# An edge MLP with segment maximum: two groups of short matmuls at other places between the tiles, and gathers held nearly one by one

## The chip, the cores and the metric

One core of a Trainium2 chip. The metric is the device time of one execution of the program, in microseconds (us); the time of the kernel before is the median of three runs.

## What is computed

A graph has N = 12500 nodes with 32 features and E = 400000 edges, sorted by their target node. Each edge takes the normalised features of its source and its target and 32 features of its own through a two-layer MLP; each node keeps the maximum of what its incoming edges give.

```python
h = jnp.maximum(_layernorm(x, axis=-1), 0.0)
e_feat = jnp.concatenate([h[src], h[dst], edge_attr], axis=-1)   # 96 wide
v = jax.nn.relu(e_feat @ W1 + b1) @ W2 + b2                      # 64, then 32
x_cand = jax.ops.segment_max(v, dst, num_segments=N)
return x + jnp.maximum(x_cand, h)
```

## The kernel before

The edges are cut into four stripes of 100000, and each stripe into 196 chunks of 512 edges; a chunk c is the same 512 positions in all four stripes. The main loop (L854) takes two chunks c and c+1 per iteration, a **pair**, through both layers, prepares the two chunks a = c+2 and b = c+3, and finishes the span products of the pair before. What TensorE (PE) does in one iteration, with the names that the profile gives (output <- operands):

- **ea**, `edges_into` (L773, ph<-ea,wt): the edge features times their part of W1, into four banks of PSUM.
- **of**, `windows_into` (L773, ph<-of,qf): what the target nodes give to layer 1, as spans of rows of q times a one-hot mask `of`, which ScalarE (ACT) builds (L641, L642). Added into the same banks.
- **ht**, `rows_into` (L773, ph<-ht,wt): the gathered source rows, transposed by VectorE (DVE), times their part of W1. Added into the same banks. ACT's relu follows (L798).
- **tr**, `leave_1` (L669): transposes of the running maxima of the pair before.
- **a1, a2, a3**, `tile` (L344, pv<-hs,hot): tiles of node spans. One in four of the source rows isn't gathered by DMA but picked by matmul: a one-hot matrix `hot` times the node features `hs`, 14 matmuls a tile; DVE masks and reduces the result (L351, L352). A chunk has four tiles, MM = 4; tile a0 was made in the iteration before, where it is called n0.
- **l2**, `second_layer` (L807).
- **lv**, `leave_2` (L686): span products, which bring the maxima of the pair before to the rows of their nodes. ACT copies one half of the result (`wo`, L692), DVE adds the other (`leave_3`, L700), and SyncE (SP) sends the stripes' rows to DRAM.
- **b0 to b3**, again L344, and in 34 of the chunks b an extra tile (pv<-hs,zero and xg), whose one-hots DVE builds late (L274).
- **n0**, tile 0 of the next pair's chunk a.

The trace holds two records for each f32 matmul of ea, of, ht and l2, so eight instructions show as x16.

GpSimd (POOL) only starts gathers: 24 indirect DMAs a pair (L179, 23 where the chunk has the extra tile), each of 128 rows of the node features from DRAM, for the pair two iterations on. POOL takes them in program order, and a table **HELD** paces them: its key is the gather's position in its pair (0 to 23), its value how many iterations back, and behind which **milestone** of PE, the gather may start. `passes` notes the matmul that is a milestone, `hold` puts the gather behind it by a semaphore, and gathers without an entry follow the one before them. In the kernel before, the table has 12 entries, two gathers to a milestone. A buffer of a gather holds three of them and there are 14; PSUM has a ring of seven banks.

Of the kernel before, what the change touches and what calls it, by code (L numbers as in the profile page):

```python
# [39 lines left out]
NCH = 196  # L40
# [6 lines left out]
A1 = 7  # L47
# [16 lines left out]
LATE = NCH - 8  # L64
PIECE = 2 * A0
GP = 3
HELD = {0: (3, 'b1'), 2: (3, 'b2'), 4: (3, 'b3'), 6: (3, 'n0'), 8: (2, 'ea'), 10: (2, 'ht'), 12: (2, 'tr'), 14: (2, 'a1'), 16: (2, 'a2'), 18: (2, 'a3'), 20: (2, 'lv'), 22: (2, 'b0')}
BANKS = 7
SOON = {(3, 0): 'a0', (3, 6): 'a2', (4, 0): 'a3', (4, 6): 'b0', (5, 0): 'b1', (5, 6): 'b2'}
ROUND = 12582912.0  # L70
# [13 lines left out]
def gnn_kernel(ctx, tc, x, src, src_mm, src_x, src_t, dst, dst_ext, lo, lo_c, ends_b, edge_attr, weights, w1, w2, b2, out):  # L84
# [129 lines left out]
    def passes(iteration, name, ins):  # L214

        passed[iteration, name] = ins

    def hold(c, i, ins):

        at = HELD.get(i + c % 2 * (K - MM))  # L220
        if at and c // 2 - at[0] >= 0:
# [9 lines left out]
    def bank(name):  # L231

        return ring[0].tile([P, C], F32, name=name, tag="bank", bufs=BANKS)
# [94 lines left out]
    def tile(c, m):  # L328

        if c not in MMC or m == MM and c not in MMX:  # L330
            return
        if m == 0:
            mm_rows[c] = early.tile([P, MM, D], F32, name="gm", bufs=4)
        if m < MM:
            hot = [hots[c][:, k, m * P:(m + 1) * P] for k in range(A1)]
            mask, row = masks[c][:, m], mm_rows[c][:, m]
        else:
            _, mask, spaces = extras.pop(c)
            hot = [spaces[k // 2][:, k % 2 * P:(k % 2 + 1) * P] for k in range(A1)]
            row = gh[c][-1][:, SOME - 1]  # L340
        po = bank("pv")[:, :D * A0]
        for k in range(A1):
            for part in range(2):
                ins = nc.tensor.matmul(po, hot[k], hs[:, part, k].rearrange("p f a -> p (f a)"),  # L344
                                 start=(k == 0 and part == 0), stop=(k == A1 - 1 and part == 1))
        if m == 0 and c % 2 == 0:
            passes(c // 2 - 2, "n0", ins)
        passes(c // 2 - 1, "ab"[c % 2] + str(m), ins)
        of_group = po.rearrange("p (f a) -> p f a", a=A0)
        one = early.tile([P, D, A0], F32, name="one", bufs=2)  # L350
        nc.vector.tensor_tensor(one, of_group, mask[:, None, :].to_broadcast([P, D, A0]), op=ALU.mult)  # L351
        nc.vector.tensor_reduce(row, one, axis=AX.X, op=ALU.max)  # L352
# [3 lines left out]
    def to_features(c, part):  # L356

        if c >= NCH or (c, part) in turned:
            return
        turned.add((c, part))  # L360
        if c not in hts:
            hts[c] = early.tile([P, K, D], F32, name="ht", bufs=4)
        ht = hts[c]
        n = min(K - MM * (c in MMC), (SE - c * C) // D)
        if part < J:
            r = slice(part * SOME, min((part + 1) * SOME, n))
            if r.start < n:
                nc.vector.transpose(ht[:, r].rearrange("p k e -> p (k e)"),  # L368
                                    gh[c][part][:, :r.stop - r.start].rearrange("p k f -> p (k f)"))
        elif c in MMC:  # L370
            nc.vector.transpose(ht[:, n:].rearrange("p k e -> p (k e)"),
                                mm_rows.pop(c).rearrange("p k f -> p (k f)"))
        else:
            for k in range(J, len(gh[c])):
                r = slice(k * SOME, min((k + 1) * SOME, n))
                nc.vector.transpose(ht[:, r].rearrange("p k e -> p (k e)"),
                                    gh[c][k][:, :r.stop - r.start].rearrange("p k f -> p (k f)"))
            if n < K:
                nc.vector.memset(ht[:, n:], 0.0)
# [183 lines left out]
    with tc.tile_pool(name="edges", bufs=3) as pool, tc.tile_pool(name="edges_ps", bufs=1, space=PSUM) as ps:  # L563
# [90 lines left out]
        def blocks(c):  # L654
            return min(J, -(-(SE - c * C) // P))
# [23 lines left out]
        def leave_2(c, sos, last):  # L679

            n = 1 + (c < NCH - 2)
            pw = bank("pv")[:, :n * 2 * P]
            pw = pw.rearrange("p (x h q) -> p x h q", x=n, h=2)
            for x in range(2):
                for j in range(blocks(c + x)):
                    ins = nc.tensor.matmul(pw[:, x % n], last[x][:, j].rearrange("p s w -> p (s w)"),  # L686
                                           sos[x][0][:, j], start=(j == 0 and x < n),
                                           stop=(j == blocks(c + x) - 1 and x >= 2 - n))
            passes(c // 2 + 1, "lv", ins)
            wo = pool.tile([P, 2, P], F32, name="wo", bufs=2)  # L690
            if c < NCH - 6:
                nc.scalar.activation(wo, pw[:, :, 0], AF.Copy)  # L692
            else:
                nc.vector.tensor_copy(wo[:, :n], pw[:, :, 0])
            return pw, wo
# [80 lines left out]
        def edges_into(c):  # L776

            ph = banks[c] = [bank("ph") for s in range(NS)]
            passes(c // 2, "ea", into_ph(ph, [(w1c, loaded[c + x][0]) for x in range(2)], True, False))
            return ph  # L780

        def windows_into(c, ph):
            of = [ofs.pop(c + x) for x in range(2)]
            q = fetched.pop(c // 2)
            into_ph(ph, [(q[:, x], of[x]) for x in range(2)], False, False)
# [40 lines left out]
        tile(2, 0)  # L826
        one_hots(3, 0, 2)
        tile(2, 1)
        one_hots(3, 2, BY_ACT.start)
        mask_of(3)  # L830
# [10 lines left out]
        ph = edges_into(0)  # L841
# [11 lines left out]
        windows_into(0, ph)  # L853
        for c in range(0, NCH - 4, 2):  # L854
            a, b = c + 2, c + 3
            if c:
                ph = edges_into(c)
                windows_into(c, ph)
            rows_into(c, ph)
            if c % LOAD:  # L860
                load_edges(c + LOAD // 2 + AHEAD)
# [7 lines left out]
            if c == LATE + 2:  # L869
                ea = pool.tile([P, LOAD * C], F32, name="ea", bufs=2)  # L870
# [3 lines left out]
            if c:  # L874
                so = [leave_1(c - 2 + x, sbs[x]) for x in range(2)]
# [15 lines left out]
                tile(a + 2, 0)  # L891
            pv = second_layer(c, hid)
            if c:
                pw = leave_2(c - 2, so, last)
            if c:
                one_hots_act(a + 2)
            load_keys(a + KEYS)
            load_key_x(b + 2)
# [7 lines left out]
            sms = [scan(c, pv[0], sm)]  # L906
            if c:
                tile(b, 0)
                to_features(b, 0)
            sms.append(scan(c + 1, pv[1], sms[0]))  # L910
            sm = sms[1]
# [10 lines left out]
            last = [lasts(c + x) for x in range(2)]  # L922
# [27 lines left out]
            tile(b, MM)  # L950
            to_features(b, 3)
            to_features(b, J)
            if a + 2 < NCH - 2:
                if c:
                    tile(a + 2, 0)
            else:
                ph = edges_into(c + 2)
                windows_into(c + 2, ph)
            if a + 2 < NCH - 2:
                to_features(a + 2, 0)  # L960
            if c == (NB - 1) * BLOCK + 2:
                bp = bank("pv")[:, 0:1]
# [31 lines left out]
        c = NCH - 4  # L994
# [5 lines left out]
        so = [leave_1(c - 2 + x, sbs[x]) for x in range(2)]  # L1000
# [6 lines left out]
        ph = edges_into(c + 2)  # L1007
        windows_into(c + 2, ph)
        pw = leave_2(c - 2, so, last)
# [4 lines left out]
        so = [leave_1(c + x, sbs[x]) for x in range(2)]  # L1014
# [9 lines left out]
        pw = leave_2(c, so, lasts_2[:2])  # L1024
# [9 lines left out]
        so = [leave_1(c + 2 + x, sbs[x]) for x in range(2)]  # L1034
# [152 lines left out]
```

## Time and profile before

| | us |
|---|---|
| runs, median (lowest, highest) | 3587.91 (3581.08, 3589.38) |
| profiled execution | 3575.96 |
| its span, first to last instruction | 3574.1 |
| PE busy | 3241.7 (91%) |
| DVE busy | 2223.2 (62%) |
| POOL busy | 2207.4 (62%) |
| ACT busy | 1578.5 (44%) |

The profile is of one execution. A row of a group gives line, engine, operation, output and operands, shape and count, then busy time and the mean of one in ns, then the idle time of the engine just before such instructions and what ended most of it. "issue" there means that the engine stood still and the profile shows nothing that it waited for. In rows by time, the first two numbers are start and length in us; a run of like instructions is one row, and brackets at its end give the idle time ahead of it. The granted clock is the share of TensorE's full clock that the chip allowed, 1.00 at full speed. Busy time of PE is modelled at its ends, since matmuls overlap.

### The profile page before, as it was taken

How to read it: one execution, taken by the hardware profiler on the slowest of the kernel's cores; microseconds unless marked ns; L12 is line 12 of the kernel's file. 1: busy time of each engine (PE TensorE's matmuls, PEld its weight loads, DVE VectorE, ACT ScalarE, POOL GpSimd, SP SyncE). 2: the span in 40 equal slices, each digit the busy share in tenths (PEclk: the TensorE clock that was granted, in tenths of full speed). 3: DMA queues.
4: the chain of work that ended last, by engine and by line, in shares of the span. 5: the costliest groups of instructions: out<-in, count | busy, mean ns of one | idle time of the engine just before them, and what ended most of it. 6: DMA issues, size and time to landing. Idle time of an engine off the chain costs nothing.

```text
span 3574.1 us, 55458 instructions
## 1 busy us (share of the span) xinstructions
PE 3241.7 (91%) x19141; PEld 2547.7 (71%) x19141; DVE 2223.2 (62%) x4215; ACT 1578.5 (44%) x2470; POOL 2207.4 (62%) x2337
## 2 busy tenths in 40 slices
PE   5899999989999998999999999989999999999987
PEld 3577777777777776777777767777777777777765
DVE  5456666666666666666666666656665666666655
ACT  3344444443534444444443434444444444444443
POOL 6666666665666666666666666666666666666662
PEclk8899999999999999999999999999999999999997
DMA  5322222222222222222222222222222222222222
GB/s 175 99 60 62 53 64 62 62 50 62 64 62 53 61 63 65 50 66 60 62 50 70 57 56 58 59 59 61 60 62 59 60 61 61 63 65 49 59 58 65
DMA packets 178819, 227.49 MB, mean 64 GB/s; under 512 B 109621, under 2 KB 150373, under 8 KB 165734
## 3 DMA queue, kind: packets, MB, share of 16 engines
q10 hardware_dynamic: 29828, 108.01, 9.6%
q0 software_dynamic: 74336, 38.21, 8.5%
q1 hardware_dynamic: 74370, 77.70, 7.0%
q8 instruction: 151, 2.47, 0.3%
q14 instruction: 134, 1.10, 0.1%
HBM read 212.23 MB, written 11.46 MB: 63 GB/s over the span
## 4 chain that ended last, share of the span: by engine, by line
PE 81%; issue 10%; DVE 6%; another core or an unknown queue 2%; SPq 1%; DMA 1%; ACT 1%; DVEq 0%; ACTq 0%
PE pv L344 60%; PE ph L773 10%; PE pv L686 4%; PE pv L669 3%; PE pv L807 3%; DVE hot L304 1%; DVE one L351 1%; DVE last L650 1%; DVE sm L815 1%; DMA top_d<-wo 0%; DVE ht L368 0%; SPq L616 0%; SPq L707 0%; SPq L625 0%
## 5 line engine op out<-in xcount | busy, mean ns | idle before, releaser
L179 POOL DMA_INDIRECT gh<-h_d,src_i x2291 | 2169.8, 947 | 1296.3 <-issue 560.0
L344 PE MATMUL pv<-hs,hot 128*128 128x448 f32 x10752 | 2373.0, 378 | 97.5 <-issue 83.9
L344 PEld LDWEIGHTS pv<-hs,hot 128*128 128x128 f32 x10752 | 2089.1, 196 | 345.7 <-issue 159.7
L351 DVE TENSOR_TENSOR one<-pv,mask 128x448 f32<-128x448 f32 x768 | 472.3, 615 | 1219.7 <-remote 464.7
L798 ACT ACTIVATE hid<-ph,wt 128x512 f32<-128x512 f32 x392 | 250.0, 688 | 1124.6 <-remote 498.2
L352 DVE TENSOR_REDUCE gm<-one 128x32 f32<-128x448 f32 x768 | 476.2, 620 | 26.5
L304 DVE TENSOR_TENSOR hot<-kb,consts 128x1024 fp32r<-128x1024 f16 (+1 forms) x379 | 447.5, 1199 | 0.0
L318 ACT ACTIVATE hot<-away,ones 128x512 fp32r<-128x512 f32 x582 | 421.6, 724 | 45.0 <-remote 26.1
L317 ACT ACTIVATE away<-kb,key_n 128x512 f32<-128x512 f16 x582 | 416.0, 715 | 0.0
L692 ACT ACTIVATE wo<-pv 128x256 f32<-128x256 f32 x95 | 36.6, 385 | 631.2 <-remote 439.2
L815 DVE TENSOR_TENSOR_SCAN sm<-pb,sm,pv 128x512 f32<-128x512 bf16 x195 | 243.6, 1249 | 16.5 <-remote 9.0
L686 PEld LDWEIGHTS pv<-so,last 128*128 128x128 f32 x768 | 107.5, 191 | 159.5 <-issue 148.5
L773 PE MATMUL ph<-ht,wt 32*64 32x512 f32 x1568 | 197.3, 618 | 21.0 <-issue 13.0
L686 PE MATMUL pv<-so,last 128*128 128x256 f32 x768 | 148.6, 304 | 74.3 <-issue 67.7
L368 DVE STREAM_TRANSPOSE ht<-gh 128x96 f32<-128x96 f32 x774 | 207.4, 269 | 1.2
L661 ACT ACTIVATE sb<-sm,wt 128x512 f32<-128x512 f32 x196 | 138.1, 715 | 138.7 <-issue 87.6
L669 PEld LDWEIGHTS pv<-ident,sb 128*128 128x128 f32 x782 | 91.8, 150 | 120.3 <-issue 95.1
L773 PE MATMUL ph<-of,qf 32*64 32x512 f32 x1552 | 147.6, 600 | 19.6 <-issue 17.5
L669 PE MATMUL pv<-ident,sb 128*128 128x128 f32 x782 | 126.4, 298 | 30.4 <-issue 24.4
L773 PEld LDWEIGHTS ph<-ht,wt 32*64 32x64 f32 x1568 | 62.7, 135 | 114.1 <-issue 98.5
L642 ACT ACTIVATE of<-of,ones 128x512 f32<-128x512 f32 x194 | 140.6, 725 | 6.3
L641 ACT ACTIVATE of<-db,below 128x512 f32<-128x512 int32 x194 | 137.4, 708 | 0.0
(115 smaller groups left out, 1328.2 us busy)
## 6 DMA issues: line engine op xcount, KB each, us to landing
ea<-in_edge_attr SPq DMA_DIRECT2D x49, 1024.0 KB
db<-in_dst_ext ACTq DMA_DIRECT2D x48, 1024.0 KB
gh<-h_d,src_i POOLq DMA_INDIRECT x2291
pb<-pen_d ACTq DMA_DIRECT2D x48, 512.0 KB
kb<-key_d ACTq DMA_DIRECT2D x47, 512.0 KB
top_d<-wo SPq DMA_DIRECT2D x752, 3.0 KB
qf<-q_d SPq DMA_DIRECT2D x392, 16.0 KB
q_d<-qs SPq DMA_DIRECT2D x6, 512.0 KB
```

The source lines that it names most:

```text
L179: ins = nc.gpsimd.indirect_dma_start(out=parts[-1][:, i, :], out_offset=None, in_=h_d[:, :], in_offset=bass.IndirectOffsetOnAxis(ap=src_i[ ...
L304: nc.vector.tensor_tensor(hot_of(c)[:, start:stop], keys[c][:, None, :].to_broadcast([P, n, MM * P]), key_ps[:, start:stop, None].to_broad ...
L317: nc.scalar.activation(away, keys[c], AF.Square, bias=key_n[:, k:k + 1])
L318: nc.scalar.activation(hot_of(c)[:, k], away, AF.Relu, bias=ones, scale=-1.0)
L344: ins = nc.tensor.matmul(po, hot[k], hs[:, part, k].rearrange("p f a -> p (f a)"), start=(k == 0 and part == 0), stop=(k == A1 - 1 and par ...
L351: nc.vector.tensor_tensor(one, of_group, mask[:, None, :].to_broadcast([P, D, A0]), op=ALU.mult)
L352: nc.vector.tensor_reduce(row, one, axis=AX.X, op=ALU.max)
L669: passes(c // 2 + 1, "tr", nc.tensor.transpose(px[:, j, :], sb[:, j * P:(j + 1) * P], ident))
L686: ins = nc.tensor.matmul(pw[:, x % n], last[x][:, j].rearrange("p s w -> p (s w)"), sos[x][0][:, j], start=(j == 0 and x < n), stop=(j == ...
L773: ins = nc.tensor.matmul(ph[s][x * HID:(x + 1) * HID], w[g], e[g], start=start, stop=stop)
L798: nc.scalar.activation(hid[k], of, AF.Relu, bias=b1c)
L815: nc.vector.tensor_tensor_scan(found[:, :n], loaded.pop(c)[2][:, :n], pv[:, :n], -LOW if before is None else before[:, C - 1:C], op0=ALU.a ...
```

## The change

Four things, with no instruction of an engine added or removed:

1. HELD goes from 12 to 21 entries: nearly every gather has a milestone of its own.
2. A tile is a milestone twice: at its end as before, and in its middle (name with "-").
3. ea and of of the next pair move from the head of an iteration to the end of the one before, ahead of n0 instead of behind it.
4. lv moves from right behind l2 to behind b0, and with it the ACT copy of its result, past the three one-hot halves (six instructions) that ACT builds for the next chunk a (`one_hots_act(a + 2)`) and the loads behind them.

Lines behind the table move by 2 and those behind `tile` by 4: L344 becomes L346, L669 L673, L686 L690, L692 L696, L773 L777, L807 L811, L179 L181.

```diff
--- before.py
+++ after.py
@@ -64,7 +64,9 @@
 LATE = NCH - 8
 PIECE = 2 * A0
 GP = 3
-HELD = {0: (3, 'b1'), 2: (3, 'b2'), 4: (3, 'b3'), 6: (3, 'n0'), 8: (2, 'ea'), 10: (2, 'ht'), 12: (2, 'tr'), 14: (2, 'a1'), 16: (2, 'a2'), 18: (2, 'a3'), 20: (2, 'lv'), 22: (2, 'b0')}
+HELD = {0: (3, 'b1'), 1: (3, 'b2-'), 2: (3, 'b2'), 3: (3, 'b3-'), 4: (3, 'b3'), 5: (2, 'ea'), 6: (3, 'n0-'),
+        7: (3, 'n0'), 9: (2, 'ht'), 10: (2, 'tr'), 12: (2, 'a1-'), 13: (2, 'a1'), 14: (2, 'a2-'), 15: (2, 'a2'),
+        16: (2, 'a3-'), 17: (2, 'a3'), 18: (2, 'l2'), 19: (2, 'b0-'), 20: (2, 'b0'), 21: (2, 'lv'), 22: (2, 'b1-')}
 BANKS = 7
 SOON = {(3, 0): 'a0', (3, 6): 'a2', (4, 0): 'a3', (4, 6): 'b0', (5, 0): 'b1', (5, 6): 'b2'}
 ROUND = 12582912.0
@@ -343,9 +345,11 @@
             for part in range(2):
                 ins = nc.tensor.matmul(po, hot[k], hs[:, part, k].rearrange("p f a -> p (f a)"),
                                  start=(k == 0 and part == 0), stop=(k == A1 - 1 and part == 1))
-        if m == 0 and c % 2 == 0:
-            passes(c // 2 - 2, "n0", ins)
-        passes(c // 2 - 1, "ab"[c % 2] + str(m), ins)
+            if k in (A1 // 2, A1 - 1):
+                at = "" if k == A1 - 1 else "-"
+                if m == 0 and c % 2 == 0:
+                    passes(c // 2 - 2, "n0" + at, ins)
+                passes(c // 2 - 1, "ab"[c % 2] + str(m) + at, ins)
         of_group = po.rearrange("p (f a) -> p f a", a=A0)
         one = early.tile([P, D, A0], F32, name="one", bufs=2)
         nc.vector.tensor_tensor(one, of_group, mask[:, None, :].to_broadcast([P, D, A0]), op=ALU.mult)
@@ -853,9 +857,6 @@
         windows_into(0, ph)
         for c in range(0, NCH - 4, 2):
             a, b = c + 2, c + 3
-            if c:
-                ph = edges_into(c)
-                windows_into(c, ph)
             rows_into(c, ph)
             if c % LOAD:
                 load_edges(c + LOAD // 2 + AHEAD)
@@ -891,8 +892,6 @@
                 tile(a + 2, 0)
             pv = second_layer(c, hid)
             if c:
-                pw = leave_2(c - 2, so, last)
-            if c:
                 one_hots_act(a + 2)
             load_keys(a + KEYS)
             load_key_x(b + 2)
@@ -906,6 +905,7 @@
             sms = [scan(c, pv[0], sm)]
             if c:
                 tile(b, 0)
+                pw = leave_2(c - 2, so, last)
                 to_features(b, 0)
             sms.append(scan(c + 1, pv[1], sms[0]))
             sm = sms[1]
@@ -950,13 +950,11 @@
             tile(b, MM)
             to_features(b, 3)
             to_features(b, J)
+            ph = edges_into(c + 2)
+            windows_into(c + 2, ph)
             if a + 2 < NCH - 2:
                 if c:
                     tile(a + 2, 0)
-            else:
-                ph = edges_into(c + 2)
-                windows_into(c + 2, ph)
-            if a + 2 < NCH - 2:
                 to_features(a + 2, 0)
             if c == (NB - 1) * BLOCK + 2:
                 bp = bank("pv")[:, 0:1]
```

On PE, one pair from tr on, up to tr of the next pair, before (64x512 is one instruction of L773; x56 is b0 to b3):

```order
L669 MATMUL pv<-ident,sb 128x128 x8
L344 MATMUL pv<-hs,hot 128x448 x42
L807 MATMUL pv<-hid,wt 32x512 x8
L686 MATMUL pv<-so,last 128x256 x8
L344 MATMUL pv<-hs,hot 128x448 x56
L344 MATMUL pv<-hs,zero 128x448 x4
L344 MATMUL pv<-hs,xg 128x448 x10
L344 MATMUL pv<-hs,hot 128x448 x14
L773 MATMUL ph<-ea,wt 64x512 x8
L773 MATMUL ph<-of,qf 64x512 x8
L773 MATMUL ph<-ht,wt 64x512 x8
L669 MATMUL pv<-ident,sb 128x128 x8
```

The same stretch after:

```order
L673 MATMUL pv<-ident,sb 128x128 x8
L346 MATMUL pv<-hs,hot 128x448 x42
L811 MATMUL pv<-hid,wt 32x512 x8
L346 MATMUL pv<-hs,hot 128x448 x14
L690 MATMUL pv<-so,last 128x256 x8
L346 MATMUL pv<-hs,hot 128x448 x42
L346 MATMUL pv<-hs,zero 128x448 x4
L346 MATMUL pv<-hs,xg 128x448 x10
L777 MATMUL ph<-ea,wt 64x512 x8
L777 MATMUL ph<-of,qf 64x512 x8
L346 MATMUL pv<-hs,hot 128x448 x14
L777 MATMUL ph<-ht,wt 64x512 x8
```

lv (L686, now L690) stands behind the first 14 of the tiles of b, and the last tile, n0, stands between of and ht instead of ahead of ea.

On ACT, where the copy wo stood before, among the six one-hot halves of an iteration (away and hot, three halves for chunk b and three for the next a):

```order
L318 ACTIVATE hot<-away,ones 128x512
L692 ACTIVATE wo<-pv 128x256
L317 ACTIVATE away<-kb,key_n 128x512
```

and after, at the end of the same six:

```order
L319 ACTIVATE away<-kb,key_n 128x512
L320 ACTIVATE hot<-away,ones 128x512
L287 DMA kb<-key_d 128x2048
L696 ACTIVATE wo<-pv 128x256
L665 ACTIVATE sb<-sm,wt 128x512 x2
```

The copy wo stood between the third half and the fourth, and stands now behind all six and behind the load of keys, ahead of the running maxima's bias (sb).

On POOL, eight gathers of a pair with what each waits for (DMASW: a queue slot of an earlier gather; DVE: its buffer; PE: a milestone), before:

```order
L179 DMA gh<-h_d,src_i 128x32 [waits DMASW2_49,DVE_49,PE_49]
L179 DMA gh<-h_d,src_i 128x32 [waits DMASW3_49]
L179 DMA gh<-h_d,src_i 128x32 [waits DMASW4_49,PE_49]
L179 DMA gh<-h_d,src_i 128x32 [waits DMASW5_49,DVE_49]
L179 DMA gh<-h_d,src_i 128x32 [waits DMASW6_49,PE_49]
L179 DMA gh<-h_d,src_i 128x32 [waits DMASW7_49]
L179 DMA gh<-h_d,src_i 128x32 [waits DMASW0_49,DVE_49,PE_49]
L179 DMA gh<-h_d,src_i 128x32 [waits DMASW1_49]
```

and after:

```order
L181 DMA gh<-h_d,src_i 128x32 [waits DMASW2_49,DVE_49,PE_49]
L181 DMA gh<-h_d,src_i 128x32 [waits DMASW3_49,PE_49]
L181 DMA gh<-h_d,src_i 128x32 [waits DMASW4_49,PE_49]
L181 DMA gh<-h_d,src_i 128x32 [waits DMASW5_49,DVE_49,PE_49]
L181 DMA gh<-h_d,src_i 128x32 [waits DMASW6_49,PE_49]
L181 DMA gh<-h_d,src_i 128x32 [waits DMASW7_49,PE_49]
L181 DMA gh<-h_d,src_i 128x32 [waits DMASW0_49,DVE_49,PE_49]
L181 DMA gh<-h_d,src_i 128x32 [waits DMASW1_49,PE_49]
```

Every gather of these now waits for PE, where every second one did.

## The prediction

> **What bounds the kernel now.** I read the page's busy times and chain first.
>
> ```profile
> PE 3241.7 (91%) x19141; PEld 2547.7 (71%) x19141; DVE 2223.2 (62%) x4215; ACT 1578.5 (44%) x2470; POOL 2207.4 (62%) x2337
> ...
> PE 81%; issue 10%; DVE 6%; another core or an unknown queue 2%; SPq 1%; DMA 1%; ACT 1%; DVEq 0%; ACTq 0%
> ...
> L179 POOL DMA_INDIRECT gh<-h_d,src_i x2291 | 2169.8, 947 | 1296.3 <-issue 560.0
> L344 PE MATMUL pv<-hs,hot 128*128 128x448 f32 x10752 | 2373.0, 378 | 97.5 <-issue 83.9
> ...
> L686 PE MATMUL pv<-so,last 128*128 128x256 f32 x768 | 148.6, 304 | 74.3 <-issue 67.7
> ```
>
> TensorE (PE) sets the end; next comes "issue", PE standing still for nothing that the profile names. The waits of PE say where:
>
> ```profile
> PE pv L344 <- issue: 90.9, 172, 2.7
> PE pv L686 <- issue: 67.7, 130, 1.1
> PE ph L773 <- issue: 40.5, 44, 14.8
> PE pv L344 <- DVE zero L274: 27.1, 15, 3.0
> PE pv L669 <- issue: 24.4, 44, 1.1
> ...
> PE pv L344 <- DVE hot L304: 12.2, 10, 2.7
> ...
> PE pv L344 <- DVE mask L323: 3.0, 2, 2.6
> ```
>
> L686 (lv, span products), L669 (tr, transposes) and L773 (ea, of, ht) are short matmuls, and lose more than their share: L686 has 768 records to L344's 10752, yet loses 67.7 us to its 90.9. (The 27.1 us for zero are the extra tile's wait for DVE in some of the pairs; the change leaves it as it is.) To see why I read one pair in PE's order of time (start, length, line, tiles, count, idle before):
>
> ```profile
> 2025.62 2.96 PE L344 MATMUL pv<-hs,hot 128*128 128x448 f32 x14
> 2028.51 1.11 PE L773 MATMUL ph<-ea,wt 32*64 32x512 f32 x16
> 2029.42 1.06 PE L773 MATMUL ph<-of,qf 32*64 32x512 f32 x16
> 2030.28 1.06 PE L773 MATMUL ph<-ht,wt 32*64 32x512 f32 x16
> 2031.27 1.09 PE L669 MATMUL pv<-ident,sb 128*128 128x128 f32 x8
> ...
> 2041.14 1.09 PE L807 MATMUL pv<-hid,wt 64*32 64x512 f32 x16
> 2042.16 0.97 PE L686 MATMUL pv<-so,last 128*128 128x256 f32 x6
> 2043.62 0.37 PE L686 MATMUL pv<-so,last 128*128 128x256 f32 x1 [0.48 <-issue]
> 2045.03 0.28 PE L686 MATMUL pv<-so,last 128*128 128x256 f32 x1 [1.04 <-issue]
> 2046.42 0.91 PE L344 MATMUL pv<-hs,hot 128*128 128x448 f32 x2 [1.11 <-issue]
> ...
> 2063.45 1.11 PE L773 MATMUL ph<-ea,wt 32*64 32x512 f32 x16
> 2065.22 2.75 PE L773 MATMUL ph<-ht,wt 32*64 32x512 f32 x16
> ```
>
> A tile of node spans takes 2.89 us (2025.62 to 2028.51), ea 0.91, of 0.86, ht 0.99, tr 0.85, l2 1.02. Here lv with b0's first matmul loses 0.48 + 1.04 + 1.11 = 2.63 us; the later ht takes 2.75 where the earlier took 1.06: 1.69 lost. Beside lv runs this on POOL:
>
> ```profile
> 2028.86 0.95 POOL L179 DMA_INDIRECT gh<-h_d,src_i  x1 [4.65 <-PE pv L344]
> ...
> 2035.01 0.94 POOL L179 DMA_INDIRECT gh<-h_d,src_i  x1 [1.46 <-remote]
> ...
> 2043.77 0.94 POOL L179 DMA_INDIRECT gh<-h_d,src_i  x1 [0.30 <-issue]
> 2046.75 0.94 POOL L179 DMA_INDIRECT gh<-h_d,src_i  x1 [2.04 <-PE pv L686]
> ```
>
> Eight gathers in a row, 0.95 + 0.30 = 1.25 us each, from 2035.01; PE is free again after the last. Another pair, PE then POOL:
>
> ```profile
> 2157.60 1.22 PE L686 MATMUL pv<-so,last 128*128 128x256 f32 x8
> 2158.66 7.59 PE L344 MATMUL pv<-hs,hot 128*128 128x448 f32 x36
> ```
>
> ```profile
> 2154.37 0.95 POOL L179 DMA_INDIRECT gh<-h_d,src_i  x1 [1.25 <-PE pv L344]
> ```
>
> POOL had paused 1.25 us shortly ahead of that lv, and it loses nothing. Of the 84 lv from 360 to 3400 us, 68 had POOL without a pause of note in the 4 us before and lost 3.05 us on average (lv with b0's first ten matmuls); 16 had a pause, and lost 0.06. First and last of the stalled, then of the clean:
>
> ```profile
> 396.01 0.86 PE L686 MATMUL pv<-so,last 128*128 128x256 f32 x5
> ...
> 3260.40 0.86 PE L686 MATMUL pv<-so,last 128*128 128x256 f32 x5
> ```
>
> ```profile
> 502.05 1.25 PE L686 MATMUL pv<-so,last 128*128 128x256 f32 x8
> ...
> 3299.03 1.22 PE L686 MATMUL pv<-so,last 128*128 128x256 f32 x8
> ```
>
> So I hold that short matmuls pile up something that a long run of gathers keeps from draining, and that a pause of POOL of about 1 us drains. The trace shows the coincidence, not the mechanism. A stall costs twice: by stretches (length; busy time of PE, PEld, DVE, ACT, POOL; granted clock),
>
> ```profile
> 2042.20:2046.40 4.20, 1.58 (x13) 1.39 (x9) 0.00 (x0) 0.00 (x0) 1.90 (x3) 0.86 0.11 16
> 2046.40:2051.00 4.60, 4.58 (x13) 4.05 (x13) 3.92 (x6) 2.79 (x5) 3.34 (x4) 0.50 0.12 20
> ```
>
> the 4.6 us behind this one run at a clock of 0.50. Over the whole run the clock is
>
> ```profile
> core 0: 3574.1 us, clock 0.944
> ```
>
> so (1 - 0.944) x 3574 = 200 us go to it, beside 90.9 + 67.7 + 25.7 + 24.4 = 208.7 us of issue waits (25.7 is 40.5 without its one wait of 14.8, a single stretch of no pair): about 1 us of clock per us of stall, if all of it follows stalls.
>
> **The change part by part.** No instruction is added or removed, so POOL still needs 24 x 1.25 = 30.0 us a pair; the pair above, 2028.51 to 2063.45, took 34.9, which leaves it 4.9 us of pauses. What changes is where they fall, and what PE does then. All terms are for some 97 pairs.
>
> 1. *The waits of tile n0 for DVE.* The 12 waits for hot and mask (15.2 us, longest 2.7) stand at n0, ahead of which DVE builds n0's one-hots. Now ea and of stand there, 0.91 + 0.86 = 1.77 us: all but the longest are covered. -14; bounds -15 and 0.
>
> 2. *Span products behind b0.* Until now 24 short matmuls in a row (l2, lv); now 16, then a tile of 2.89 us, then 8. Records per time fall, but POOL is no freer. By the new holds each half tile (1.44 us) releases one gather (1.25), so POOL works off 0.2 us per half tile; what n0, ht and tr release (gathers 7 to 11, 6.25 us, within the 0.99 + 0.85 + 1.44 = 3.3 us to the middle of a1) leaves 3 us of backlog, and through l2 and b0 POOL still runs without a pause. I take about half of L686's 67.7, because the burst is split and not relieved: -35. Bounds: -68 (all gone) and +68 (lv stalls alike, and b0 behind l2 anew).
>
> 3. *ht and tr.* They now follow n0, not of. b3, ea and the middle of n0 release one gather each, 3.75 us, in 0.91 + 0.86 + 1.44 + 1.44 = 4.6 us from b3's end to n0's, so POOL pauses just ahead of them. Half of L773's 25.7 and L669's 24.4: -25; bounds -50 and 0.
>
> 4. *ea and of.* They leave the end of n0 for the end of b3, where gathers 22, 23 and 0 to 4, 7 x 1.25 = 8.75 us, are released over the 7.2 us from the middle of b1 to b3's end: no pause ahead of them. The nearest row is the stalled ht, 1.69 us; 97 of these would be +164, none 0. Today L773 waits 44 times, several to a burst, so about one burst in four of one kind; one in four here is 24 x 1.69 = +41. ACT's span masks for of are early enough to be read 2.89 us sooner; the last of the pair above ended at 2018.55, 10.9 us ahead of its matmuls:
>
> ```profile
> 2017.82 0.73 ACT L642 ACTIVATE of<-of,ones 128x512 f32<-128x512 f32 x1
> ```
>
> 5. *ACT, SP and the holds.* The copy of the span products (L692) now stands behind three more one-hot halves on ACT, which idled ahead of it before:
>
> ```profile
> L692 ACT ACTIVATE wo<-pv 128x256 f32<-128x256 f32 x95 | 36.6, 385 | 631.2 <-remote 439.2
> ```
>
> 631.2 / 95 = 6.6 us of idle a pair covers the tile by which it is later; behind it ACT's next work waits for scan anyway. Without that cover, 0.4 us x 97 = +37. The nine more holds put a wait on gathers that run with 0.30 us between them whether they have one or not: 0, and if a late release opens a gap, POOL has 4.9 us. Stripe writes on SP come a tile later, and nothing reads them soon: 0.
>
> 6. *Clock.* Issue stalls change by -35 - 25 + 41 = -19; at half of the 1 to 1 above, since not all slow stretches need follow a stall, -9. Bounds: what the bounds of 2 to 4 give, times 1.
>
> Sum: -14 - 35 - 25 + 41 - 9 = -42 us: the profiled execution, 3576.0 (span 3574.1), becomes 3534. The median of the runs shown, 3587.9, is 12 above that execution; 3587.9 - 42 = 3546.
>
> [...]
>
> **Rivals.**
>
> *Slower: ea and of become the new lv.* Seven gathers without a pause lie ahead of them, as ahead of the stalled lv. If 7 pairs in 10 lose 1.69 us, that is 68 x 1.69 = +115 in place of +41; with -14 - 35 - 25 it is +41, and with the clock at half (+28 for a net stall of +55) +69, 3657; at 5 in 10 (+82: stalls +22, clock +11) +19, 3607. It decides from some 41 pairs of 97 on, where 1.69 us and half as much clock outweigh the rest. For it: the arithmetic of 4. Against: all of L773 together, three kinds of burst, loses 25.7 us now. Chance 0.23.
>
> *Nothing: the pauses only move.* POOL's 30.0 us a pair are fixed, so what PE gains is taken from the 4.9 us of pauses, and the stall comes at another place: what 2 and 3 gain, 4 loses. Only n0's waits are left, offset by small late releases: 3578 to 3599, about 3588. For it: POOL's share. Against: 16 lv show that a pause of 1.25 us at the right place is enough. Chance 0.13.
>
> *Much faster: single gathers drain.* If the small rests between singly held gathers suffice, 67.7 + 25.7 + 24.4 = 118 go, the 14, and half as much clock, 59: -191, 3397. For it: the clean lv. Against: the rests are 0.2 us in the sum of 2, and 0.30 us between gathers does not help today. Chance 0.10.
>
> **How the numbers follow.** Forecast, with mixed terms: 0.54, own range 3500 to 3575. About 0.3%, 11 us, can be told from no change, so 3577 to 3599 is "same". Faster: 0.54 + 0.10 = 0.64; same 0.13; slower 0.23. The range leaves out the much faster case and the upper half of the slower one, some 2 in 10: 3480 to 3635.
>
> **What would show it.** Right: L690 (was L686) with issue waits near 33 us, L777's at ht and L673's halved, no wait for hot at n0, the clock at 0.95 or more, and ea or of with some new waits. Step 2 is wrong if l2 or b0 now stalls for what lv lost; step 4 if L777's issue waits at ea and of pass 80 us. If POOL is as unbroken ahead of lv as before and lv is still clean, the mechanism itself is not the run of gathers.

## The result and the profile after

The changed kernel takes 3579.36 us (median of 20 runs, 3570.19 to 3605.11), the kernel before 3581.23 in the same measurement (20 runs): ratio 1.0002, 95% interval 0.9989 to 1.0015. **No change**, where -42 us was forecast.

One thing has to be said ahead of the rest. Measurements came in two kinds of session. In nine of them, the one above among these, the kernel before took 3570 to 3620 us; in three it took 3004 us, and one and the same chip showed 3620 in one and 3004 in another. I call them *stalling* and *quiet* sessions. Kernels are compared only with the kernel before in their own session; the trace of before that the prediction reads is of the stalling kind. In each of the nine, one kernel ran beside the kernel before, and in the three quiet ones two or four did; whether that has to do with it no run tells. The two kinds differ ahead of the main loop already: its first full pair begins at 75 to 77 us in the traces of quiet sessions, and at 96 to 112 in those of stalling ones.

The page of the changed kernel, its clock, and the waits of PE:

```profile
PE 3292.8 (92%) x19141; PEld 2500.2 (70%) x19141; DVE 2222.8 (62%) x4215; ACT 1582.7 (44%) x2470; POOL 2208.1 (62%) x2337
```

```profile
core 0: 3575.2 us, clock 0.963
```

```profile
PE pv L346 <- issue: 83.2, 135, 5.5
PE ph L777 <- issue: 59.3, 89, 6.6
PE pv L690 <- issue: 38.9, 58, 1.8
...
PE pv L346 <- DVE mask L325: 8.7, 2, 4.3
...
PE pv L346 <- DVE hot L306: 4.3, 4, 1.5
```

L690's waits went from 67.7 to 38.9 us, tr's 24.4 are gone, and the clock rose from 0.944 to 0.963: (1 - 0.963) x 3575 = 132 us instead of 200. Yet the span is the same, and PE is *busier* by 51 us with the same instructions. The groups say where. Before, then after:

```profile
L773 PE MATMUL ph<-of,qf 32*64 32x512 f32 x1552 | 147.6, 600 | 19.6 <-issue 17.5
```

```profile
L777 PE MATMUL ph<-of,qf 32*64 32x512 f32 x1552 | 232.5, 644 | 32.3 <-issue 29.3
```

Busy time of `of` grew by 85 us for the same matmuls, its waits for "issue" by 12 (17.5 to 29.3): most of what these matmuls lose stands in busy records, not in waits. PE in order of time shows it, with l2, b0, lv, b1 to b3, ea, of, n0, ht:

```profile
2047.61 1.09 PE L811 MATMUL pv<-hid,wt 64*32 64x512 f32 x16
2048.63 2.36 PE L346 MATMUL pv<-hs,hot 128*128 128x448 f32 x10
2051.57 0.65 PE L346 MATMUL pv<-hs,hot 128*128 128x448 f32 x2 [0.58 <-issue]
2052.99 0.56 PE L346 MATMUL pv<-hs,hot 128*128 128x448 f32 x2 [0.78 <-issue]
2053.40 1.11 PE L690 MATMUL pv<-so,last 128*128 128x256 f32 x8
2054.35 8.82 PE L346 MATMUL pv<-hs,hot 128*128 128x448 f32 x42
2063.10 1.11 PE L777 MATMUL ph<-ea,wt 32*64 32x512 f32 x16
2064.01 1.76 PE L777 MATMUL ph<-of,qf 32*64 32x512 f32 x8
2066.55 1.17 PE L777 MATMUL ph<-of,qf 32*64 32x512 f32 x8 [0.78 <-issue]
2067.65 3.09 PE L346 MATMUL pv<-hs,hot 128*128 128x448 f32 x14
```

and POOL beside it:

```profile
2059.33 0.95 POOL L181 DMA_INDIRECT gh<-h_d,src_i  x1 [1.33 <-PE pv L346]
...
2064.34 0.95 POOL L181 DMA_INDIRECT gh<-h_d,src_i  x1 [0.30 <-issue]
2066.82 0.95 POOL L181 DMA_INDIRECT gh<-h_d,src_i  x1 [1.53 <-remote]
```

lv is clean in this pair, but b0 takes 4.77 us behind l2 (2048.63 to 2053.40) where a tile takes 2.9, and of takes 3.64 us (2064.01 to 2067.65) instead of 0.86, at the end of a run of five gathers, free again when POOL pauses. Note also that gathers still go in runs, 1.25 us apart, though almost every one has a hold of its own: 4.8 to a run on average from 500 to 2700 us, where before had 5.1.

The prediction's count of lv comes out otherwise now. From 360 to 3400 us, taking a pause to be over 0.6 us, the kernel before has 17 lv with a pause of POOL in the 4 us ahead, and none of them loses over half a us (lv with the ten matmuls behind it). The changed kernel has 45 such lv, and 19 lose that; 12 of the 19 had four gathers started since the pause.

For a balance I took, from first matmul to first matmul, what each stretch of a pair takes, mean of the pairs between 500 and 2700 us (about 60, in quiet sessions 72). The last two rows are quiet sessions: the kernel before with half of its gathers (it runs at the time of the kernel before there) and the changed kernel.

| us a pair | ea, of | ht, tr | a1-a3 | l2 | lv | b0-b3, extra, n0 | pair |
|---|---|---|---|---|---|---|---|
| before | 2.08 | 3.21 | 9.25 | 1.12 | 2.37 | 17.81 | 35.84 |
| after | 3.91 | 2.65 | 8.80 | 1.32 | 1.48 | 17.82 | 35.97 |
| half_before_2, quiet | 1.77 | 1.84 | 8.84 | 1.02 | 1.06 | 15.71 | 30.25 |
| after_3, quiet | 1.90 | 1.89 | 8.58 | 1.02 | 0.95 | 15.99 | 30.34 |

Times 97 pairs: ea and of +178 us; ht, tr and a1 to a3 -98; lv -86, l2 +19; the other tiles +1. What one side gains the other gives back.

### The profile page after: what moved, and what is told of

Same layout as the page of the kernel before. It is cut to its first block, busy times and chain, and to the rows that moved or that the text cites. A ratio compares the mean times of both kernels' runs of the same rounds, so it can differ in the third digit from the quotient of the medians.

```text
span 3575.2 us, 55820 instructions
## 1 busy us (share of the span) xinstructions
PE 3292.8 (92%) x19141; PEld 2500.2 (70%) x19141; DVE 2222.8 (62%) x4215; ACT 1582.7 (44%) x2470; POOL 2208.1 (62%) x2337
## 3 DMA queue, kind: packets, MB, share of 16 engines
q8 instruction: 150, 2.46, 0.3%
## 5 line engine op out<-in xcount | busy, mean ns | idle before, releaser
L181 POOL DMA_INDIRECT gh<-h_d,src_i x2291 | 2170.4, 947 | 1300.8 <-issue 490.1
L346 PE MATMUL pv<-hs,hot 128*128 128x448 f32 x10752 | 2353.1, 374 | 77.8 <-issue 71.6
L346 PEld LDWEIGHTS pv<-hs,hot 128*128 128x128 f32 x10752 | 2027.7, 192 | 451.1 <-issue 178.1
L802 ACT ACTIVATE hid<-ph,wt 128x512 f32<-128x512 f32 x392 | 242.2, 689 | 1171.2 <-PE ph L777 916.8
L777 PE MATMUL ph<-of,qf 32*64 32x512 f32 x1552 | 232.5, 644 | 32.3 <-issue 29.3
L777 PE MATMUL ph<-ea,wt 32*64 32x512 f32 x1568 | 171.6, 623 | 24.3 <-issue 20.7
L777 PE MATMUL ph<-ht,wt 32*64 32x512 f32 x1568 | 168.9, 631 | 15.3 <-issue 9.3
L777 PEld LDWEIGHTS ph<-of,qf 32*64 32x64 f32 x1552 | 70.7, 135 | 140.5 <-issue 134.7
L690 PE MATMUL pv<-so,last 128*128 128x256 f32 x768 | 120.1, 287 | 39.3 <-issue 38.9
L673 PEld LDWEIGHTS pv<-ident,sb 128*128 128x128 f32 x782 | 88.7, 147 | 88.3 <-issue 45.9
L690 PEld LDWEIGHTS pv<-so,last 128*128 128x128 f32 x768 | 109.2, 190 | 47.7 <-issue 44.5
L696 ACT ACTIVATE wo<-pv 128x256 f32<-128x256 f32 x95 | 36.5, 385 | 229.0 <-PE pv L690 70.0
```

The costliest lines, as they stand in the source:

```text
L181: ins = nc.gpsimd.indirect_dma_start(out=parts[-1][:, i, :], out_offset=None, in_=h_d[:, :], in_offset=bass.IndirectOffsetOnAxis(ap=src_i[ ...
L777: ins = nc.tensor.matmul(ph[s][x * HID:(x + 1) * HID], w[g], e[g], start=start, stop=stop)
L802: nc.scalar.activation(hid[k], of, AF.Relu, bias=b1c)
```

## The experiments

Three things were open: whether gathers make the stalls, what each part of the change does alone, and whether the parts add up. Two theories went ahead: A, bursts stall where gathers ran before them, and the parts cancel; B, the loss per pair is set by the gathers and only changes its place.

**Both kernels with half of the gathers** (half_before, half_after). Half of each chunk's gathered source rows are zeros here, and the MLP's input with them.

```diff
         for k in range(0, n, SOME):
+            if c in MMC and k // SOME % 2 == 0:
+                parts.append(none)
+                continue
```

> The kernel before with half of the gathers left out: of the four buffers of three rows that a chunk takes, the first and the third are a constant of zeros and issue no gather; matmuls, transposes and all else stay. POOL then runs three gathers at a time with room between. If runs of gathers are what holds PE up, the issue waits of L344, L686, L669 and L773 (209 us together before) fall under 50, the clock rises over 0.98, and the time falls by 150 to 350 us, to 3230 to 3430. If PE stalls for its own reasons (its queue, the shape of the short matmuls, instruction fetch), waits and time stay within 50 us.

> The changed kernel with the same half of the gathers left out. If the two orders differ only in which bursts meet a run of gathers, both halved kernels come within 15 us of each other, the changed one ahead by the waits of n0 for DVE (up to 15 us). If the new order has a cost of its own (a change of matmul shape more, a bank that comes free late), the changed one is 20 us or more behind.

(`none` is a constant of zeros.) The session was quiet: before 3004.67, half_before 3004.23 (ratio 1.0002, 0.9993 to 1.0012), half_after 3028.0 (1.0077, 1.006 to 1.0093). Where nothing stalls, half of the gathers are worth nothing. The second expectation's rival came out: the new order has a cost of its own, some 23 us, told below. The first was put again, and met a quiet session again (half_before_2, chip as in after_again: 3004.35 against 3003.66, ratio 0.9999, 0.9990 to 1.0008), and then a stalling one:

> The kernel before with half of the gathers left out (the first and third buffer of a chunk are a constant of zeros). On a chip with stalls: if runs of gathers hold PE up, issue waits under 50 us and a time of 3010 to 3250; if the stalls have nothing to do with gathers, within 50 us of before. On a chip without stalls: as before, 3004.

> The kernel before with half of the gathers left out (the first and third buffer of a chunk are a constant of zeros), once more: one chip gave the kernel before 3620 us with issue waits in one session and 3004 without them in another, so what the gathers do has to be seen in a session with stalls. With stalls: if runs of gathers hold PE up, the issue waits fall under 50 us and the time to 3010 to 3250; if the stalls have nothing to do with gathers, within 50 us of before. In a session without stalls: as before, 3004.

half_before_3: 3025.39 against 3615.91 of before, ratio 0.8366 (0.8352 to 0.8380). The clock, and the waits of PE (L349 is the tiles, L778 ea, of and ht):

```profile
core 0: 3024.9 us, clock 0.988
```

```profile
PE ph L778 <- issue: 9.2, 1, 9.2
...
PE pv L349 <- issue: 7.9, 8, 1.7
```

The 209 us of issue waits are down to 18 (with 1.2 at tr), and 16 of these lie in the first 107 us, where most gathers still go back to back; the clock is 0.988, where the trace of before has 0.944. From 500 to 2700 us a pair takes 30.28 us, as half_before_2's 30.25: in the loop nothing of the loss is left. That the full load of gathers holds PE up in a stalling session is shown; the zeros alone don't explain it, since the same edit changes nothing in a quiet one. By what way isn't shown: the edit leaves fewer gathers and also longer pauses of POOL. And gathers aren't enough: below, a quiet session has all of them, hardly a pause of POOL, and no stall.

**The parts, in a quiet session** (lv_only, edges_only, order_only, holds_only; chip and session one and the same):

lv_only has the move of `leave_2`, order_only this and the next:

```diff
             pv = second_layer(c, hid)
-            if c:
-                pw = leave_2(c - 2, so, last)
...
                 tile(b, 0)
+                pw = leave_2(c - 2, so, last)
-HELD = {..., 20: (2, 'lv'), 22: (2, 'b0')}
+HELD = {..., 20: (2, 'b0-'), 22: (2, 'lv')}
```

edges_only has the move of ea and of, order_only this too:

```diff
+            ph = edges_into(c + 2)
+            windows_into(c + 2, ph)
             if a + 2 < NCH - 2:
                 if c:
                     tile(a + 2, 0)
-HELD = {..., 6: (3, 'n0'), 8: (2, 'ea'), ...}
+HELD = {..., 6: (3, 'n0-'), 8: (3, 'n0'), ...}
```

holds_only leaves the order alone and has the 21 holds, with names that fit the old order:

```diff
+HELD = {0: (3, 'b1'), 1: (3, 'b2-'), 2: (3, 'b2'), 3: (3, 'b3-'), 4: (3, 'b3'), 5: (3, 'n0-'), 6: (3, 'n0'),
+        7: (2, 'ea'), 9: (2, 'ht'), 10: (2, 'tr'), 12: (2, 'a1-'), 13: (2, 'a1'), 14: (2, 'a2-'), 15: (2, 'a2'),
+        16: (2, 'a3-'), 17: (2, 'a3'), 18: (2, 'l2'), 19: (2, 'lv'), 20: (2, 'b0-'), 21: (2, 'b0'), 22: (2, 'b1-')}
```

> Span products moved behind b0, all else in the old place, and the old twelve holds (the two near them renamed to the milestones that now lie at the same distance: gather 20 behind the middle of b0, 22 behind lv). Theory A, the parts cancel: a burst of short matmuls stalls where a long run of gathers lies ahead of it, and splitting the burst of l2 and lv relieves it; the trace of the changed kernel has lv, b0 and b1 lose some 116 us less than before, so this part alone gives 60 to 130 us: 3450 to 3520. Theory B, the loss is conserved: the gathers of a pair cost PE about the same wherever the bursts stand, so this part alone is within 15 us of the kernel before, and the stalls show at ht, tr or a1.

> Only ea and of moved ahead of n0; span products behind l2 as before; twelve holds, two of them renamed to the nearest milestones in time (6 behind the middle of n0, 8 behind its end). Theory A: ea, of and n0 lose some 170 us more and ht, tr and a1 some 90 less, as the trace of the changed kernel has it, and the lv burst stalls as before: slower by 40 to 110 us, 3620 to 3690. Theory B: within 15 us of the kernel before.

> Both moves of matmuls, with twelve holds in pairs of gathers as before, at the nearest milestones of the new order. Theory A with holds that do nothing: same as the changed kernel within 15 us, 3565 to 3595. Rival: the single holds are what makes the new order bearable, and without them it is slower by 40 us or more.

> The old order of matmuls with 21 single holds at milestones as far behind as in the changed kernel, and milestones in mid-tile. If single holds make more and smaller rests of POOL, which drain, L686's issue waits (67.7 us before) fall under 40 us and the time by 40 us or more. If the news of a milestone reaches POOL late while gathers run, the gathers still go in runs of 4 to 8, and the time is within 15 us of before.

Against 3004.04: lv_only 2961.81 (0.985, 0.9837 to 0.9862), edges_only 3008.26 (1.0006, 0.9997 to 1.0015), order_only 3012.56 (1.0009, 0.9993 to 1.0025), holds_only 3004.14 (0.9997, 0.9988 to 1.0006). What had been expected of them was for a kernel before that stalls, and could not be tested here. lv_only and edges_only were repeated in the session of after_3, with the same outcome:

> The span products' move alone, again, since chips turned out to differ: two give the kernel before 3004 us without an issue wait, the first and one more 3580 to 3620 with them. On a chip with stalls: theory A (a burst stalls where a run of gathers lies ahead of it, and the two parts of the change cancel) gives 60 to 130 us less than before; theory B (the loss per pair is conserved and moves to the next burst) within 15 us. On a chip without: 42 us less, as in the first run.

> The move of ea and of alone. On a chip with stalls: theory A 40 to 110 us more than before, theory B within 15 us. On a chip without: within 5 us of before.

> The changed kernel beside its parts on one chip. On a chip with stalls: within 10 us of before, as twice so far. On one without: 3000 to 3030, no gain, since both moves together with the old holds gave 3013 there; 2955 to 2970 if the parts add up.

lv_only_2 2961.41 against 3003.66 (0.9855, 0.9840 to 0.9869), edges_only_2 3005.69 (1.0007, 0.9998 to 1.0016), after_3 3011.83 (1.0009, 0.9993 to 1.0026). The medians of order_only and after_3 lie 8 us above before's and their ratios nearer to 1, since a quarter to a third of their runs took only 2993 to 3001 us.

No theory of stalls can explain lv_only's 42 us, since PE is never held up here. Stretch 500 to 2700 us of lv_only_2, then of after_3 (length; busy time and instructions of PE, PEld, DVE, ACT, POOL; granted clock):

```profile
500.00:2700.00 2200.00, 2200.00 (x14613) 1834.37 (x14612) 1679.45 (x3167) 1166.76 (x1845) 1661.00 (x1759) 1.00 0.28 72
```

```profile
500.00:2700.00 2200.00, 2200.00 (x14332) 1784.44 (x14332) 1652.32 (x3109) 1145.55 (x1812) 1625.75 (x1722) 1.00 0.28 71
```

PE is busy throughout, and, since busy alone proves little, no matmul in these stretches or in half_before_2's starts over 0.52 us after the one before it. Yet POOL hardly pauses: lv_only_2's 1759 gathers at 1.25 us come to 2199 of the 2200 us, with three pauses of over 0.6 us, and after_3 has 0.67 a pair, where the stalling before had 4.66. That is the last of the prediction's signs: POOL is unbroken and lv is clean (0.96 and 0.95 us a pair), so a long run of gathers is not by itself what holds PE up. It also means that a PE faster than lv_only's would find the gathers in its way.

lv_only's gain is in the pace of the tiles. half_before_2, then lv_only_2:

```profile
2002.43 8.91 PE L349 MATMUL pv<-hs,hot 128*128 128x448 f32 x42
...
2013.36 14.62 PE L349 MATMUL pv<-hs,hot 128*128 128x448 f32 x70
```

```profile
2001.81 8.91 PE L344 MATMUL pv<-hs,hot 128*128 128x448 f32 x42
...
2015.54 8.56 PE L344 MATMUL pv<-hs,hot 128*128 128x448 f32 x42
```

The 42 matmuls of b1 to b3 in lv_only_2 take 8.56 us, those of a1 to a3 in both 8.91: 200 ns from one to the next instead of 207. Each of these rows fits one pace within 0.1 us: 69 steps of 207 ns make 14.28 of the 14.62 us, 41 of 200 make 8.20 of the 8.56, and 41 of 207 make 8.49 of the 8.91, the rest being the last matmul. The pair fell from 30.25 to 29.78 us, 0.47; 7 ns x 70 matmuls of b0 to b3 and n0 are 0.49 (lv gains 0.10 besides, and b0's first matmul, which now follows l2, takes it back). In order_only and after_3 it is a1 to a3 that run at 200 and the others at 207. What chooses the pace I did not find. In stalling sessions the paces are mixed: of the tile matmuls that follow at one of the two, 59 in 100 do so at 200 in before, 59 in the changed kernel, 50 to 57 in the other runs but holds_only_2, against 4 in half_before_2 and 65 in lv_only_2.

Second, the cost of n0 between of and ht, in after_3:

```profile
2003.43 1.06 PE L777 MATMUL ph<-of,qf 32*64 32x512 f32 x16
2004.42 3.15 PE L346 MATMUL pv<-hs,hot 128*128 128x448 f32 x14
2007.50 1.11 PE L777 MATMUL ph<-ht,wt 32*64 32x512 f32 x16
2008.55 1.09 PE L673 MATMUL pv<-ident,sb 128*128 128x128 f32 x8
```

of takes 0.99 instead of 0.86, ht 1.05 instead of 1.00, n0 3.08 instead of 2.98: 0.28 us a pair, 27 us in all, with two more changes a pair between a tile of 128 rows and a matmul of 32. The trace shows the time and not what makes it. edges_only has the same 0.99 and 1.05 us for of and ht and has it back, since half of its tile matmuls run at 200 (56 in 11.37 us in the pair read).

**The changed kernel once more.**

> The changed kernel once more, beside the kernel before on the same chip, since the parts of the change ran where the kernel before takes 3004 us and shows no issue waits. If there too the body is PE's own stream, the time is worked out from the parts: span products behind b0 alone gained 1.5 percent by a pace of 200 instead of 207 ns a matmul in five of eight tiles, and both moves together gave 3013; so 3000 to 3030, no gain. If the parts add up (1.5 percent less for one, nothing for the other), 2955 to 2970. If this chip stalls as in the first runs, 3560 to 3610.

A stalling session: 3621.65 against 3620.21 (1.0007, 0.9992 to 1.0023), no change again, and 12 us above the upper end expected. Its profile has ea and of at 3.97 us a pair and lv at 1.77, much as the first (3.91 and 1.48).

**The parts, in stalling sessions**, each beside the kernel before:

> The span products' move alone with twelve holds, for a session with stalls (before at 3580 to 3620). Theory A (bursts stall where gathers ran before them; the parts of the change cancel): 60 to 130 us less than before. Theory B (the loss per pair is set by the gathers and only changes its place): within 15 us of before, and what lv and b1 lose less, ea, ht, tr and a1 lose more. Without stalls: 42 us less.

3545.55 against 3576.83, ratio 0.9911 (0.9894 to 0.9927): 31 us, between the two theories. It isn't the quiet session's gain in pace: 53 in 100 of its tile matmuls run at 200, against 59 in before. The waits (L688 is lv, L671 tr, L344 the tiles):

```profile
PE pv L344 <- issue: 120.1, 209, 3.9
PE pv L671 <- issue: 48.6, 89, 1.1
...
PE pv L688 <- issue: 9.1, 14, 1.1
```

lv's waits fell from 67.7 us to 9.1, but tr's rose from 24.4 to 48.6 and the tiles' from 90.9 to 120.1. Both theories hold in part: the burst is relieved, and by the waits most of the loss turns up at the next ones; by the time about half.

> The move of ea and of alone with twelve holds, for a session with stalls. The span products' move alone gave 31 us less. If the two moves cancel: 20 to 60 us more than before. If the move costs nothing and the holds take the gain away: within 10 us of before. Without stalls: within 5 us of before.

3582.43 against 3571.71, 1.0037 (1.0021 to 1.0052): 11 us slower, between the two expectations. ea and of lose here 3.05 us a pair (2.08 before), ht and tr 2.26 (3.21).

> Both moves with twelve paired holds, for a session with stalls. If the moves add up, -0.5 percent (some 19 us less than before), and then the 21 holds cost what the whole change lacks. If the moves disturb each other and the holds do nothing: within 0.2 percent of before, as the whole change. Without stalls: 3013, as in the first run.

3543.86 against 3569.94, 0.9922 (0.9905 to 0.9940): -0.78 percent where the two add up to -0.52. So the moves together are good by 26 us, and ea and of take 2.60 us.

> The old order with 21 single holds, for a session with stalls. If the holds cost what the sum of the moves leaves open: +0.3 to +0.7 percent. If a milestone's news comes too late for single holds to act: within 0.2 percent of before, and gathers still in runs. If single holds make rests that drain, as the much faster rival had it: over 1 percent less than before. Without stalls: as before.

3540.65 against 3572.61, 0.9914 (0.9897 to 0.9930): 32 us faster, which none of the three expectations had. The waits:

```profile
PE pv L346 <- issue: 74.6, 154, 4.0
PE ph L777 <- issue: 54.7, 78, 7.2
...
PE pv L690 <- issue: 22.3, 48, 1.1
```

lv's waits fall to a third without lv having moved. POOL rested more often: 5.00 pauses of over 0.6 us a pair, mean 1.47 us, against 4.66 of 1.65 before. Single holds do act, by a little. Some of the 32 us is pace: 75 in 100 of its tile matmuls run at 200, where before had 59, worth about 0.16 x 112 x 7 ns = 0.12 us a pair, 12 us in all (an estimate; the trace of before is of another session).

So in a stalling session each half of the change is worth 0.8 to 0.9 percent, and both together nothing. Of the pairs of before, 20 percent lose over half a us at ea and of; with the moves and paired holds 34; with the moves and single holds 77, at 2.5 us each. It isn't the holds alone, though: with paired holds and the move of ea and of by itself it is some 60 (edges_only_3, 1.8 us each). I took the single holds at b1 to b3, ahead of ea, for the culprit:

```diff
-HELD = {0: (3, 'b1'), 1: (3, 'b2-'), 2: (3, 'b2'), 3: (3, 'b3-'), 4: (3, 'b3'), 5: (2, 'ea'), 6: (3, 'n0-'),
+HELD = {0: (3, 'b1'), 2: (3, 'b2'), 4: (3, 'b3'), 6: (3, 'n0-'),
```

> The changed kernel with gathers 0 to 6 held in pairs as before (b1, b2, b3, middle of n0), all others singly. If single holds at b1 to b3 keep POOL busy up to ea and so make of and n0 stall: of's loss falls from 187 us to about 100 (its value with paired holds) and the time to 0.6 to 1.6 percent below the kernel before. If the gains simply don't add, since the stall always finds a burst: within 0.3 percent of before. Without stalls: 3013.

3648.79 against 3620.35, 1.0081 (1.0057 to 1.0105): slower, and ea and of rise to 4.47 us.

```profile
PE pv L346 <- issue: 110.0, 158, 5.9
PE ph L777 <- issue: 69.1, 90, 8.2
PE pv L690 <- issue: 55.4, 88, 1.7
```

My reading was wrong. after_pairs_b differs from order_only_2 in nothing but the holds of gathers 7 to 22, and is 0.81 percent slower than before where order_only_2 is 0.78 faster, each in its own session. So it is the later holds that make ea and of stall in this order (4.47 us a pair against 2.60); which of them, no run tells.

Last, `leave_2` moved as in lv_only, with the holds of holds_only but for three:

```diff
-        16: (2, 'a3-'), 17: (2, 'a3'), 18: (2, 'l2'), 19: (2, 'lv'), 20: (2, 'b0-'), 21: (2, 'b0'), 22: (2, 'b1-')}
+        16: (2, 'a3-'), 17: (2, 'a3'), 18: (2, 'l2'), 19: (2, 'b0-'), 20: (2, 'b0'), 21: (2, 'lv'), 22: (2, 'b1-')}
```

> The span products' move and 21 single holds, ea and of in the old place behind n0. If the edge move under single holds is what takes the gain away: -1.2 to -1.9 percent against before. If any two of the parts take from each other because the stall finds the next burst (here ht, tr and a1): -0.3 to -0.9 percent. Without stalls: 2961, if the holds do nothing there.

3536.22 against 3575.97, 0.9892 (0.9873 to 0.9912), 40 us less, between the two expectations, and the lowest ratio of a kernel with all its gathers in a stalling session (its interval overlaps those of the next three). Again less than the sum of its parts (-1.75 percent): lv takes 1.20 us a pair, but ht and tr 4.48 where before had 3.21.

| us a pair, stalling | ea, of | ht, tr | a1-a3 | l2 | lv | b0-b3, extra, n0 | pair |
|---|---|---|---|---|---|---|---|
| lv_only_3 | 2.15 | 3.83 | 9.55 | 1.02 | 1.23 | 17.70 | 35.49 |
| edges_only_3 | 3.05 | 2.26 | 9.34 | 2.47 | 1.27 | 17.26 | 35.66 |
| order_only_2 | 2.60 | 2.29 | 8.96 | 2.42 | 1.16 | 18.04 | 35.46 |
| holds_only_2 | 2.46 | 4.37 | 9.47 | 1.02 | 1.52 | 16.55 | 35.39 |
| lv_new_holds | 2.58 | 4.48 | 9.53 | 1.06 | 1.20 | 16.48 | 35.33 |
| after_pairs_b | 4.47 | 2.29 | 8.77 | 1.16 | 1.81 | 18.30 | 36.80 |

Between kernels single columns move by up to 2 us; the pair stays within 35.3 to 36.8, 5 us and more over the 30.25 of a quiet session. The loss goes when half of the gathers go (30.28 in half_before_3); what the moves and holds do to it is mostly to move it.

## Why the prediction was wrong

The reading of the bound was right for a stalling session: the full load of gathers holds PE up there, half of it hardly (18 us of issue waits in half_before_3, 209 in before), and bursts of short matmuls pay (lv 2.37 us a pair in before, 1.06 in half_before_2). That an unbroken run of gathers does it, and a pause undoes it, is not borne out: the changed kernel has stalled lv behind pauses (19 of 45), and quiet sessions have unbroken gathers and no stall (lv_only_2: three pauses from 500 to 2700 us, lv at 0.96 us a pair). The rival that came true in its number is the second, "the pauses only move", which had 0.13; the first had ea and of right, 7 pairs in 10, and the gains elsewhere too small. Most signs of being right came out too (L690 at 38.9, no wait for hot at n0, the clock over 0.95), and the time did not move. Step by step:

1. *n0's waits for DVE*, -14: the row was misread. By time, 7 of the 12 waits (7.8 us) stand at n0, and 5 (7.4 us) at the extra tile. n0's are gone, as forecast, but all of the 4.3 + 8.7 = 13.0 us that are left stand ahead of the extra tile. Net about -2.
2. *Span products behind b0*, -35: lv -86, l2 +19. Right in direction, too small, and b0 now pays at times, as above.
3. *ht and tr*, -25: -54, and with a1 to a3 -98, four times as much.
4. *ea and of*, +41: **the step that failed.** It was the frequency: one pair in four at 1.69 us, read off the waits of today's bursts. Measured: 77 in 100 at 2.5 us, +178. The text had the reason for the large end before it, seven gathers without a pause ahead of ea as ahead of the stalled lv, and set it aside for a count of waits in another order of work. One in four was about right for the old place (20 in 100); it did not carry over to the new one. Its price was too low by its nature, since issue waits hold only part of the loss: in before, ea to tr lose (2.08 - 1.77) + (3.21 - 1.84) = 1.68 us a pair against half_before_2, 163 us in all, and their issue waits come to 25.7 + 24.4. The sign set for this step stayed silent for the same reason: ea and of have 20.7 + 29.3 = 50.0 us of issue waits, under the 80. Why they stall so often there stays open; the later single holds have a part in it (after_pairs_b).
5. *ACT and holds*, 0: the copy wo keeps 229 us of idle ahead of it, so ACT was no matter. But holds were costed at nothing, and alone they gain 0.86 percent, and take the gain of the moves away.
6. *Clock*, -9: the clock's loss fell from 200 to 132 us, and the time didn't. The price wasn't the same either: 0.96 us of clock per us of issue wait in before (200 to 208.7), 0.73 after (132 to 83.2 + 59.3 + 38.9 = 181.4). The lost time went into busy records: PE is busy for 51 us more.
7. *n0 between of and ht*, 0: the sum has no term for it. From start to start, of, n0 and ht take 0.28 us a pair more in after_3 than in half_before_2, 27 us in all, in a quiet session.

The steps were also added up as if each burst's stall stood for itself. lv_only_3 shows that it doesn't: 59 us fewer waits at lv than in the trace of before, 31 us less in all.

## What to carry to other kernels

In the stalling sessions here, a burst that was moved out of the way left much of its loss to the next ones (lv_only_3: 59 us fewer waits at lv, 53 more at tr and the tiles). So where one engine's traffic holds another up, price the whole cycle, and test by thinning the traffic before moving work about. Read a stall from start to start, not from idle time alone, since a hold-up may stand in busy records (`of` after the change: 85 us more busy, 12 more of waits). And price the parts of a change in both combinations: here two that gained 0.78 and 0.86 percent gave nothing together (ratio 1.0002).

## What the runs showed of the hardware

The kernel before took 3620 us in one session and 3004 in another on the same chip, a fifth less. The changed kernel's traces from these two show PE held up for nothing that the profile names in the one (ea and of 3.97 us a pair) and not in the other (1.90), with POOL's gathers nearly unbroken in the latter (0.67 pauses a pair, where the stalling before had 4.66); what differs between sessions stays open. With half of the gathers, a stalling session's pair takes 30.28 us, as a quiet one's (30.25). In a quiet session, tiles run at 200 or 207 ns a matmul, rows of 42 in 8.56 or 8.91 us, which made 42 us of difference for a move of eight matmuls a pair. With n0 between of and ht, these three take 0.28 us more a pair there.
